# Exponentials in sixteen pieces with the maximum as bias, and masks on ScalarE, in layers 0 and 2 of a four-layer graph attention kernel

## The chip, the core and the metric

The kernel runs on one core of a Trainium2 chip. The metric is the time of one launch on the device, in microseconds (us). A core has five engines with a queue each: TensorE (PE in the profile; its weight loads are PEld), VectorE (DVE), ScalarE (ACT), GpSimd (POOL) and SyncE (SP, which here only issues transfers). Each engine works through its own queue in order and waits on semaphores for the others. All data here are float32 but for the masks, which are bytes.

## The reference

The input x holds 128 graphs of 64 nodes with 512 features; adj says which nodes are neighbours. Four layers follow each other, each on relu(layernorm(x)) and each added to x. Layers 0 and 2 are the same function with their own weights: four heads of 64, attention limited to neighbours.

```python
def _L0_gnn_ref(x, adjacency_mask, Wq, Wk, Wv, Wo, bo):
    q = split_heads(x @ Wq)
    k = split_heads(x @ Wk)
    v = split_heads(x @ Wv)
    sim = jnp.einsum('bhid,bhjd->bhij', q, k) * scale          # scale = 64 ** -0.5 = 0.125
    neg = -jnp.finfo(sim.dtype).max
    sim = jnp.where(adjacency_mask[:, None, :, :], sim, neg)
    attn = jax.nn.softmax(sim, axis=-1)
    out = jnp.einsum('bhij,bhjd->bhid', attn, v)
    return out @ Wo + bo
...
h = jnp.maximum(_layernorm(x, axis=-1), 0.0)
x = x + _L0_gnn_ref(h, adj, L0_gnn_Wq, L0_gnn_Wk, L0_gnn_Wv, L0_gnn_Wo, L0_gnn_bo)
```

Layer 1 is such an attention with eight heads, a second layernorm and a mask that always keeps the diagonal. Layer 3 multiplies the softmax by a mask of cosine similarities over 0.1 and uses eight heads; its last stage is another. The change touches neither's arithmetic.

## The kernel before, in words

**Tiles and steps.** The 8192 rows (graph, node) are cut into 16 steps of 512 rows: four blocks of 128 rows, each holding two graphs of 64 nodes. The kernel runs over layer by layer, and within a layer step by step, so there are 64 (layer, step) pairs. Between layers x lies in DRAM.

**Stages of one step of layer 0 or 2.** SP loads x into `xin` (L486). `scales` and `normalize` make the layernorm: DVE takes statistics (L443, L445), adds epsilon (L448), POOL takes the power -1/2 (L450), DVE makes the bias (L452), ACT applies it (L459). PE transposes 128x128 squares into `ptr` (L570) and ACT copies them into `hT` (L574). Products with weights are done by Strassen's scheme in Winograd's form (`winograd`): seven products of half-size blocks instead of eight, with sums of blocks made ahead (`sums_of_b`, L363 on DVE and L366 on POOL). All its matmuls stand at L613, into the PSUM banks `mA`, `mB` and `mC`. What comes out of a bank is taken away by `Out` or `Residual`: ACT copies (L630, L650, and L1040 into a buffer `u`), DVE adds (L643, L654), POOL adds (L1045). A product may overwrite a bank only once the copy out of it is done, so PE waits for such copies.

**The attention.** `scores` (L930) multiplies the heads' q and k in 64x64 quarters into the tile `sc`, which fills two PSUM banks: 128 partitions (two graphs of 64 queries) by 1024 (16 groups of 64 keys: four heads, four blocks). Then `softmax_parts`:

- DVE overwrites the non-neighbours with a very negative number (L941, a predicated copy whose mask is the tile `n`, with 1 where there is no edge);
- DVE takes the maximum of each group of 64 (L947) into `mx`, 128x16;
- DVE subtracts it (L949) from the scores into the SBUF tile `E`; with this `sc` is free (`se.set()`);
- ACT takes exp(0.125 E) in place, one operation of 1024 (L952);
- DVE sums each group (L959), takes the reciprocal (L963), and POOL multiplies (L965).

`transposed` turns `E` (eight ACT copies at L974 and one DVE transpose at L979), `attention` multiplies it by v into `po` (L1097). The scores `sc` and `po` share one buffer of two PSUM banks (`r_sc`, a ring of 1), so po of one step can be written only once `sc` of the next is released. ACT copies `po` out (L1106), DVE makes the sums for the product with `Wo` (L363), and the seven products of `Wo` are added to `xres`, which holds x plus the bias vector (L1024), and stored (L1065).

**Masks.** `masks` runs once for each step: SP loads 128x256 bytes of adj (L988); in layers 0 and 2 DVE makes `n` = (adj == 0) at L1005. Layer 1 also takes out the diagonal (L1002), layer 3 has another form (L996).

**What sets the order.** No queue is written by hand. Every stage is a Python generator that yields what its next instruction will cost, for example `yield dve(1.2)` or `yield act(1.06)`, before it records it. The class `Order` keeps a clock for each engine and always lets the generator go on whose instruction can start first by these figures. Two rules bend this: streams carry a priority, and on ACT and DVE a stream of priority 0 (the copies that empty PSUM banks) that would become ready before a longer operation ends goes ahead of it (`urgent`). So the figures in the yields fix the order of the instructions on every engine; the chip then runs each queue in that order, and where real lengths differ from the figures an instruction waits in its place. A changed figure or a new operation can thus move instructions everywhere.

Rings and banks limit how far a stage can run ahead: `E` has two buffers, adj and `n` two each, the small tile pool `soft` (for `mx` and the sums) three, `u` four, `xres` two, `mA` and the pair `mB`/`mC` two each.

**Lines that the change and the prediction touch:** `softmax_parts` (L934 to L955), `masks` (L983 to L1007), `softmax` (L1191), and around them L443 to L459 (layernorm), L613 (matmuls), L630, L650, L1040 (ACT copies), L643 (DVE adds), L1045 and L366 (POOL), L486, L988, L1020 (loads by SP).

Of the kernel before, what the change touches and what calls it, by code (L numbers as in the profile page):

```python
# [8 lines left out]
F32 = mybir.dt.float32  # L9
U8 = mybir.dt.uint8  # L10
AF = mybir.ActivationFunctionType
ALU = mybir.AluOpType
AX = mybir.AxisListType

P = 128
D = 512
N = 64
# [194 lines left out]
def dve(us):  # L212
    return ("dve", us, 0.1)


def act(us):
    return ("act", us, 0.1)
# [6 lines left out]
def load(us=2.2):  # L224
    return ("sp", 0.6, us)
# [3 lines left out]
def gnn_stack(ctx: ExitStack, tc: tile.TileContext, a: dict, out: bass.AP):  # L229
    nc = tc.nc  # L230
# [12 lines left out]
    const = ctx.enter_context(tc.tile_pool(name="const", bufs=1))  # L243
# [43 lines left out]
    sel = const.tile([P, 32], F32, name="sel")  # L287
    nc.vector.memset(sel, 0.0)

    bdw = const.tile([P, P], F32, name="bdw")  # L290
    nc.vector.memset(bdw, 0.0)
    for g in range(2):
# [638 lines left out]
                                         lT[r, c, k], rT[r, c, k], start=True, stop=True)  # L931
        return S, e

    def softmax_parts(S, se, E, mask, neg, masked):  # L934

        m = mask.rearrange("p b k -> p (b k)")
        n = m.shape[1]
        sv = S.rearrange("p a (c m) -> p (a c) m", m=n)
        shape = [P, 1024 // n, n]
        yield dve(1.5)  # L940
        nc.vector.copy_predicated(sv, m[:, None, :].to_broadcast(shape),  # L941
                                  negs[:, neg:neg + 1, None].to_broadcast(shape))
        masked.set()
        S3 = S.rearrange("p a (i k) -> p (a i) k", k=N)
        mx = soft.tile([P, 16], F32, tag="mx", name="mx")
        yield dve(1.2)
        nc.vector.tensor_reduce(mx, S3, AX.X, ALU.max)  # L947
        yield dve(1.2)
        nc.vector.tensor_tensor(E, S3, mx[:, :, None].to_broadcast([P, 16, N]), ALU.subtract)  # L949
        se.set()  # L950
        yield act(1.06)
        nc.scalar.activation(E, E, AF.Exp, scale=0.125)  # L952
        sm = soft.tile([P, 2, 16], F32, tag="sm", name="sm")
        yield from row_sums(sm[:, 0, :], E)
        return sm  # L955

    def row_sums(o, E):
        yield dve(1.2)
        nc.vector.tensor_reduce(o, E, AX.X, ALU.add)  # L959

    def divide(E, sm):
        yield dve(0.24)
        nc.vector.reciprocal(sm, sm)  # L963
        yield pool(1.95)
        nc.gpsimd.tensor_mul(E, E, sm[:, :, None].to_broadcast([P, 16, N]))  # L965
# [17 lines left out]
    def masks(l, s):  # L983

        adj, ae = yield from r_adj.new()
        n = TB * N
        yield load(3.5)
        nc.sync.dma_start(adj.rearrange("p b k -> p (b k)"), a["adj"][:, s * n:(s + 1) * n])  # L988
        n0, ne = yield from r_n0.new()
        if l == 3:  # L990
            nz = small.tile([P, TB], U8, tag="nz", name="nz", bufs=1)
            yield dve(0.3)
            nc.vector.tensor_scalar(nz, adj[:, :, 0], 0.0, None, ALU.is_equal)

            yield dve(0.6)
            nc.vector.scalar_tensor_tensor(n0, adj, 0.0, nz[:, :, None].to_broadcast([P, TB, N]),  # L996
                                           ALU.is_equal, ALU.mult)
            return adj, ae, n0, ne
        yield dve(0.6)
        if l == 1:  # L1000

            nc.vector.scalar_tensor_tensor(n0, adj, 0.0, noteye[:, None, :].to_broadcast(  # L1002
                [P, TB, N]), ALU.is_equal, ALU.mult)
        else:
            nc.vector.tensor_scalar(n0, adj, 0.0, None, ALU.is_equal)  # L1005
        ae.set()
        return n0, ne, None, None  # L1007
# [150 lines left out]
    def front(l, s):  # L1158

        mask, me, nf, nfe = yield from masks(l, s)  # L1160
        yield s_ready[l, s]
        z = st[l, s]
# [6 lines left out]
        for u, blocks in enumerate(units):  # L1169
            E, e = yield from r_e.new("E")  # L1170
            S, se = yield from scores(z["q"], z["k"], 2 * nch, blocks)
            if u == len(units) - 1:
                for n in ("q", "k", "qk"):
                    if f"{n}_done" in z:
                        z[f"{n}_done"].set()
            m = mask[:, blocks[0]:blocks[0] + len(blocks)]
            z["e", u], z["exp", u] = (E, e), od.event()
            od.spawn(softmax(l, z, u, S, se, m, masked[u]), 1)
# [11 lines left out]

    def softmax(l, z, u, S, se, m, masked):  # L1191
        E = z["e", u][0]
        sm = yield from softmax_parts(S, se, E, m, (0, 1, 0, 2)[l], masked)
        z["sm", u] = sm
        if l < 3:
            yield from divide(E, sm[:, 0, :])
            z["e_ready", u].set()
        z["exp", u].set()
# [136 lines left out]
```

## Time and profile before

| | us |
|---|---|
| median of three runs (lowest, highest) | 2790.13 (2788.91, 2795.86) |
| the profiled execution, its own time | 2791.22 |
| its span, from the first to the last instruction | 2789.2 |
| layer 0 without its start and end: window 40 to 470 | 430 |
| layer 1: window 510 to 1300 | 790 |
| layer 2: window 1385 to 1850 | 465 |
| layer 3: window 1900 to 2700 | 800 |

The granted clock of TensorE in this execution is 0.993 of full speed. The DMA engines are busy between a tenth and a half of the time in each fortieth of the span.

How to read the views: the busy totals give, for each engine, the time in which it worked, the share of the span and the number of instructions. The chain of work that ended last is followed back from the last instruction, each time to what released it. A group's row names line, engine, operation, output and input, their shapes and the number of instructions; then the busy time, the mean length of one in ns, and the idle time of the engine just before them with what ended it. The view of waits says who waited for whom: us in total, how often, the longest. The windows give the busy time of each engine within a stretch; the last three columns there are the granted clock, the share of the DMA engines and GB/s. In the timeline the columns are the start, the length, the engine, and in square brackets the idle time before with its releaser.

### The profile page before, as it was taken

Reading aid. Unit: us, or ns where it says so; the run is one execution under the profiler, and the core shown is the slowest. Engines: PE = TensorE matmul, PEld = TensorE weight load, DVE = VectorE, ACT = ScalarE, POOL = GpSimd, SP = SyncE. Lnnn points to the kernel's source line nnn. Section 1 sums busy time; section 2 is a strip of 40 time slices with the busy share of each in tenths; the row PEclk is TensorE's granted clock in tenths of the full one; section 3 lists DMA queues with packets and bytes.
Section 4 is the critical chain, followed back from the end, with each engine's and each line's share of the span. In section 5 each row is a group of like instructions: output and inputs, shape, how many; then the busy total and the mean of one; then the engine's idle time right before and its main releaser. Section 6 shows DMA issues by size and latency. Waiting matters only on the chain.

```text
span 2789.2 us, 63654 instructions
## 1 busy us (share of the span) xinstructions
PE 2723.9 (98%) x26728; PEld 2362.1 (85%) x26728; DVE 1896.2 (68%) x2780; ACT 1872.4 (67%) x3149; POOL 1608.2 (58%) x1242
## 2 busy tenths in 40 slices
PE   8999999999999999999999999999999999999997
PEld 7888888888888888888888888878888888888876
DVE  6766767677767667766657666746777667776656
ACT  5756756688777777776656656657566776677644
POOL 5667667645435445446656576676665656555543
PEclk9999999999999999999999999999999999999998
DMA  4333333212112111112322242332422233223221
GB/s 157 108 107 109 108 116 114 96 63 77 47 62 77 47 61 64 61 47 97 122 93 92 93 138 93 108 104 78 111 64 63 71 93 86 64 63 84 73 63 47
DMA packets 160430, 238.51 MB, mean 86 GB/s; under 512 B 23952, under 2 KB 69008, under 8 KB 160144
## 3 DMA queue, kind: packets, MB, share of 16 engines
q1 hardware_dynamic: 145632, 219.98, 25.4%
q10 hardware_dynamic: 14512, 14.47, 1.6%
q8 instruction: 210, 3.44, 0.5%
q14 instruction: 76, 0.62, 0.1%
HBM read 166.77 MB, written 67.63 MB: 84 GB/s over the span
## 4 chain that ended last, share of the span: by engine, by line
PE 91%; DVE 4%; POOL 2%; ACT 1%; issue 1%; DMA 1%; POOLq 0%; SPq 0%; ACTq 0%; DVEq 0%
PE mA L613 46%; PE mC L613 23%; PE mB L613 12%; PE sc L930 5%; PE po L1097 2%; PE ptr L570 2%; PE po L1242 1%; PE mmn L872 1%; POOL xres L1045 1%; POOL xres L1024 1%; ACT F L974 1%; DVE xres L643 1%; DVE E L949 0%; DVE t L363 0%; POOL E L965 0%
## 5 line engine op out<-in xcount | busy, mean ns | idle before, releaser
L974 ACT COPY F<-E 32x512 f32<-32x512 f32 x768 | 472.5, 615 | 41.0 <-POOL E L965 26.3
L1045 POOL TENSOR_TENSOR xres<-xres,u 128x512 f32<-128x512 f32 x192 | 259.9, 1361 | 296.3 <-ACT u L1040 236.1
L1024 POOL TENSOR_TENSOR xres<-xres,u 128x512 f32<-128x512 f32 x192 | 260.8, 1380 | 23.0 <-DMA xres<-x 17.0
L366 POOL TENSOR_TENSOR t<-hT 128x512 f32<-128x512 f32 x126 | 181.4, 1440 | 145.7 <-DVE hT L544 89.0
L459 ACT ACTIVATE xin<-xin,rs 128x512 f32<-128x512 f32 x320 | 247.8, 810 | 19.4 <-DVE rs L452 15.6
L630 ACT COPY v<-mA 128x256 f32<-128x256 f32 (+1 forms) x192 | 92.0, 479 | 218.5 <-PE mA L613 205.5
L534 ACT COPY t<-xin 32x512 f32<-32x512 f32 x364 | 224.1, 616 | 6.4
L450 POOL TENSOR_TENSOR rs<-rs,mhalf 128x2 f32<-128x2 f32 x160 | 115.9, 726 | 192.0 <-DVE rs L448 168.7
L443 DVE BATCH_NORM_STATS2 st<-xin 128x6 f32<-128x512 f32 x320 | 214.9, 672 | 15.8 <-DMA xin<-in_x 7.7
L613 PE MATMUL mA<-w_vo,t 128*128 128x128 f32 (+1 forms) x1152 | 204.5, 312 | 1.1 <-ACT u L1040 1.1
L613 PE MATMUL mA<-t,w_qk 128*128 128x256 f32 x768 | 185.9, 381 | 1.5 <-DVE t L363 1.5
L965 POOL TENSOR_TENSOR E<-E,sm 128x1024 f32<-128x1024 f32 x64 | 127.8, 1997 | 100.6 <-DVE sm L963 87.3
L613 PE MATMUL mA<-t,w_q 128*128 128x256 f32 x744 | 179.2, 383 | 0.0
L613 PEld LDWEIGHTS mA<-w_vo,t 128*128 128x128 f32 x1152 | 166.2, 191 | 14.6 <-ACT u L1040 4.3
L613 PE MATMUL mA<-t,w_k 128*128 128x256 f32 x744 | 177.3, 381 | 0.0
L366 POOL TENSOR_TENSOR t<-hT,t 128x512 f32<-128x512 f32 x126 | 168.3, 1336 | 7.7 <-DVE hT L544 4.2
L959 DVE TENSOR_REDUCE sm<-E 128x16 f32<-128x1024 f32 x128 | 154.9, 1210 | 12.8 <-ACT E L952 12.1
L613 PEld LDWEIGHTS mA<-t,w_qk 128*128 128x128 f32 x768 | 144.4, 192 | 20.3 <-DVE t L363 1.7
L613 PEld LDWEIGHTS mA<-t,w_q 128*128 128x128 f32 x744 | 140.5, 191 | 20.8 <-issue 1.2
L613 PEld LDWEIGHTS mA<-t,w_k 128*128 128x128 f32 x744 | 140.3, 190 | 19.4
L979 DVE STREAM_TRANSPOSE pt<-F 128x1024 f32<-128x1024 f32 x96 | 118.7, 1236 | 49.8 <-ACT F L974 49.6
L1040 ACT COPY u<-mA 128x512 f32<-128x512 f32 x144 | 84.4, 586 | 97.7 <-PE mA L613 88.8
(217 smaller groups left out, 6908.9 us busy)
## 6 DMA issues: line engine op xcount, KB each, us to landing
x<-xres SPq DMA_DIRECT2D x96, 512.0 KB
xin<-x SPq DMA_DIRECT2D x96, 512.0 KB
xres<-x SPq DMA_DIRECT2D x64, 512.0 KB
xres<-in_x SPq DMA_DIRECT2D x32, 512.0 KB
u<-rs SPq DMA_DIRECT2D x128, 128.0 KB
xres<-x SPq DMA_DIRECT2D x64, 256.0 KB
out<-xres SPq DMA_DIRECT2D x64, 256.0 KB
xin<-in_x SPq DMA_DIRECT2D x30, 512.0 KB
```

What stands on the lines that cost most here:

```text
L366: nc.gpsimd.tensor_tensor(o, i0, i1, ALU.subtract)
L443: nc.vector.bn_stats(st, v[:, t, :])
L459: nc.scalar.activation(v[:, t, :], v[:, t, :], func, bias=rs[:, 2, t:t + 1], scale=rs[:, 0, t:t + 1])
L534: nc.scalar.copy(o, v)
L613: nc.tensor.matmul(o, l, r, start=(first and m == 0 and k == 0), stop=(k == KC - 1), skip_group_check=True)
L930: nc.tensor.matmul(S[g * N:(g + 1) * N, par, col], lT[r, c, k], rT[r, c, k], start=True, stop=True)
L959: nc.vector.tensor_reduce(o, E, AX.X, ALU.add)
L965: nc.gpsimd.tensor_mul(E, E, sm[:, :, None].to_broadcast([P, 16, N]))
L974: nc.scalar.copy(F[g * N + 32 * k:g * N + 32 * (k + 1), :, 32 * i:32 * (i + 1)], E[g * N + 32 * i:g * N + 32 * (i + 1), :, 32 * k:32 * (k ...
L979: nc.vector.transpose(o, F)
L1024: nc.gpsimd.tensor_add(xr[:, t, :], xr[:, t, :], bo[l])
L1045: nc.gpsimd.tensor_add(v, v, both(u))
```

## The change

In layers 0 and 2, and only there:

- the subtraction of the maximum is left out. Instead the maximum is multiplied by -0.125 in place (128x16), and ACT takes exp(0.125 S - 0.125 max) straight from the scores' banks, in 16 operations of 64 columns each, since a bias is one number for each partition and each group of 64 has its own. The scores' banks are released after the last of these;
- the mask is made by ACT as 1 - adj, with a bias tile `ones` and scale -1, instead of by DVE's comparison.

The figures given to the planner are 0.1 for the scaling, 0.21 for each exp and 0.4 for the mask.

```diff
+    ones = const.tile([P, 1], F32, name="ones")
+    nc.vector.memset(ones, 1.0)
...
-    def softmax_parts(S, se, E, mask, neg, masked):
+    def softmax_parts(S, se, E, mask, neg, masked, narrow=False):
...
         nc.vector.tensor_reduce(mx, S3, AX.X, ALU.max)
-        yield dve(1.2)
-        nc.vector.tensor_tensor(E, S3, mx[:, :, None].to_broadcast([P, 16, N]), ALU.subtract)
-        se.set()
-        yield act(1.06)
-        nc.scalar.activation(E, E, AF.Exp, scale=0.125)
+        if narrow:
+            yield dve(0.1)
+            nc.vector.tensor_scalar(mx, mx, -0.125, None, ALU.mult)
+            for i in range(16):
+                yield act(0.21)
+                nc.scalar.activation(E[:, i, :], S3[:, i, :], AF.Exp, bias=mx[:, i:i + 1], scale=0.125)
+            se.set()
+        else:
+            yield dve(1.2)
+            nc.vector.tensor_tensor(E, S3, mx[:, :, None].to_broadcast([P, 16, N]), ALU.subtract)
+            se.set()
+            yield act(1.06)
+            nc.scalar.activation(E, E, AF.Exp, scale=0.125)
...
+        if l != 1:
+
+            yield act(0.4)
+            nc.scalar.activation(n0, adj, AF.Identity, bias=ones, scale=-1.0)
+            ae.set()
+            return n0, ne, None, None
         yield dve(0.6)
         if l == 1:
...
-        sm = yield from softmax_parts(S, se, E, m, (0, 1, 0, 2)[l], masked)
+        sm = yield from softmax_parts(S, se, E, m, (0, 1, 0, 2)[l], masked, l in (0, 2))
```

The branch for layer 3 in `masks` returns before the new one, so `l != 1` there means layers 0 and 2. The matmuls, their number and their operands are the same in both kernels.

## The prediction

> **What bounds the kernel now.** I read the busy totals and the chain first, then the windows by layer, then what the tensor engine (PE) waits for in layers 0 and 2, then the rows of the operations that the change touches, and last one step of the timeline.
>
> Busy totals and the chain that ended last, from the page:
>
> ```profile
> PE 2723.9 (98%) x26728; PEld 2362.1 (85%) x26728; DVE 1896.2 (68%) x2780; ACT 1872.4 (67%) x3149; POOL 1608.2 (58%) x1242
> ...
> PE 91%; DVE 4%; POOL 2%; ACT 1%; issue 1%; DMA 1%; POOLq 0%; SPq 0%; ACTq 0%; DVEq 0%
> ```
>
> PE is idle for 65 us in all. The change removes no matmul, so it can win only what PE stands idle, and only in layers 0 and 2. Those windows (layer 0, layer 1, layer 2; columns: length, then busy us and count for PE, weight loads, DVE, ACT, POOL):
>
> ```profile
> 40.00:470.00 430.00, 420.67 (x4128) 375.57 (x4127) 306.63 (x484) 281.45 (x476) 290.40 (x225) 1.00 0.34 111
> ...
> 510.00:1300.00 790.00, 789.70 (x7153) 683.55 (x7152) 546.80 (x813) 610.96 (x945) 383.65 (x318) 1.00 0.19 63
> ...
> 1385.00:1850.00 465.00, 451.23 (x4285) 401.62 (x4287) 310.95 (x491) 287.62 (x492) 298.14 (x233) 0.99 0.31 105
> ```
>
> PE idles 9.3 us in the layer 0 window and 13.8 us in the layer 2 window, 23.1 us together: 0.72 us for each of 32 steps. Who ends those waits (0 to 480 us, then 1300 to 1880 us):
>
> ```profile
> PE mC L613 <- DVE xres L643: 3.6, 2, 1.8
> PE mB L613 <- DVE xres L643: 2.6, 2, 1.3
> PE po L1097 <- DVE E L949: 2.4, 3, 1.0
> ```
>
> ```profile
> PE mC L613 <- DVE xres L643: 5.3, 2, 3.5
> PE po L1097 <- DVE pt L979: 3.0, 2, 2.8
> PE po L1097 <- DVE E L949: 2.5, 3, 1.1
> ```
>
> Only the L949 lines (4.9 us) are the operation that the change takes away. ACT is 62 to 65% busy there, DVE 67 to 71%: neither is a bound, so only order and lateness matter. Groups of the operations concerned, shapes apart:
>
> ```profile
> L949 DVE TENSOR_TENSOR E<-sc,mx 128x1024 f32<-128x1024 f32 x96 | 117.0, 1219 | 1.8
> L952 ACT ACTIVATE E<-E 128x1024 f32<-128x1024 f32 x96 | 101.5, 1057 | 9.4 <-DVE E L949 8.9
> L634 ACT ACTIVATE kT<-mA,vecs 128x256 f32<-128x256 f32 x96 | 40.3, 471 | 27.6 <-PE mA L613 26.7
> L448 DVE TENSOR_SCALAR rs<-mv 128x2 f32<-128x2 f32 x160 | 66.2, 414 | 5.0
> L1005 DVE TENSOR_SCALAR n<-adj 128x256 uint8<-128x256 uint8 x32 | 17.5, 547 | 1.3 <-DMA adj<-in_adj 1.3
> ```
>
> One softmax of layer 0 in the timeline (start, length):
>
> ```profile
> 163.56 0.37 ACT L630 COPY v<-mA 128x256 f32<-128x256 f32 x1 [0.18 <-PE mA L613]
> 163.83 1.52 ACT L459 ACTIVATE xin<-xin,rs 128x512 f32<-128x512 f32 x2
> 164.68 1.23 DVE L941 COPY_PREDICATED sc<-n,negs 128x1024 f32<-128x1024 uint8 x1 [1.77 <-PE sc L930]
> 165.95 1.22 DVE L947 TENSOR_REDUCE mx<-sc 128x16 f32<-128x1024 f32 x1
> 167.44 1.22 DVE L949 TENSOR_TENSOR E<-sc,mx 128x1024 f32<-128x1024 f32 x1
> ```
>
> ACT's next instruction starts 0.27 us after a 0.37 us copy: lengths overlap by 0.1, so occupancy is read from starts.
>
> **What the Trainium skill says.** "ScalarE: Activation LUTs", What ACT_TABLE_LOAD costs: an ACTIVATE takes 186 ns + 0.833 ns per element, each pointer operand (here the bias) adds about 93 ns, and back-to-back ones overlap by about 93 ns. The trace agrees on slope ((586-372)/256 = 0.836 ns, copies of 512 and 256) and overlap. "SBUF — State Buffer", Who interferes with whom: a tensor_scalar in a two-port mode and GpSimd exclude each other for a whole instruction. The trace agrees: L448 takes 0.17 us in the median and up to 1.85, L1005 0.285 and up to 1.28. "PSUM — Partial Sum Buffer", Engine vs sequencer instructions: ScalarE's queue is strict first in, first out, so an exp that waits holds every copy behind it.
>
> **The change part by part**, per step, 16 steps in each of two layers.
>
> 1. The subtraction goes: DVE -1.22 us. Also its 4.9 us of PE waits.
>
> 2. One exp of 1024 (length 1.06, occupancy about 0.95) becomes 16 of 64 out of PSUM with a bias. No row shows that. L634 is the nearest: pointer bias, PSUM, 256 wide, two in 0.84 us, so 0.84-0.47 = 0.37 us apart. Less 192 x 0.836 ns: 0.21 us. Upper end: if they don't overlap, 0.471-0.160 = 0.31. I take 0.21, because the pairs of L634 do overlap: 3.4 us, or ACT +2.4 us. At 0.31 it is 5.0.
>
> 3. The maximum is scaled by -0.125: one TENSOR_SCALAR on 128x16. From L448: 0.17 alone, up to about 1.3 if POOL has just begun an operation (its rows here last 1.3 to 1.4). It lies between maximum and first exp.
>
> 4. The mask moves to ACT: DVE -0.55 (mean of L1005), ACT +0.4 (256 x 0.833 ns and, by the page, two times 93 ns; 0.5 if nothing overlaps).
>
> 5. The scores' bank stays held until the last exp instead of the end of the subtraction (4.0 us after the scores: 168.66-164.62).
>
> Sum: ACT +2.8 us per step, 90 us in all; DVE about -1.4 per step. At some 28.4 us per step ACT goes to about 75%. Nothing of this is on PE by itself; what counts is the order.
>
> The kernel's planner lays every queue out anew, and the new order repeats identically over 24 of the 32 steps (11 in layer 0, 13 in layer 2); layers 1 and 3 keep theirs but at their edges. So I follow one repeating step with measured lengths, zero at the end of the scores. PE start to start: product of Wo 0.87, of V 0.89, scores or po 1.09 (timeline: 179.08 to 179.94, 165.04 to 165.93, 163.46 to 164.55). After the scores PE runs five Wo products and half a V product to 4.80, the other half to 5.25, then the last Wo product, four V products and half of one to 10.12, then po. Results are readable about 0.2 later.
>
> ACT after the scores: two copies of u, exp x2, copy u (fifth Wo product, readable 4.1), mask, exp, copy V, exp x10, copy V, exp, copy V, exp x2. PE's last Wo product, due at 5.25, waits for that third u, which is now **behind two exps**, and these behind the scaled maximum.
>
> DVE: predicated copy 0.1 to 1.4; then xres<-mB, which by its semaphore waits for POOL's addition of the first u, which stands behind a POOL sum of hT; then maximum, then scale. POOL: sum to about 0.3, addition to 1.6, so xres 1.7 to 2.4, maximum to 3.6; scale waits for POOL's operation then running, to about 4.3; first exp 4.45. Then u is copied 4.9 to 5.45: PE stalls **0.2 us**. If the predicated copy (two SBUF inputs, 1.2 to 2.3 us in its rows) and POOL's addition take turns instead, the addition ends at 2.8, the maximum at 4.8, the scale at 5.5; first exp 5.6, u at 6.6: **1.35 us**. Both ends are open; I take the middle, 0.75.
>
> Behind it, from the first exp e: V copies are due at PE's pace, and ten exps at 0.21 put the second at e+3.9, where its product is readable at e+3.85; the last exp ends at e+5.5, po's turn is e+5.9. So part 5 and the long exp run cost nothing at 0.21. At 0.31 the ten cost 1.0 us more, of which 0.27 is slack: 0.75 us of stall.
>
> The mask's wait: SP issues its load 0.9 us behind that of xin, which waits for the last transposes, about -1.9. Halves of xin land 3.6 to 4.6 and 4.9 to 5.9 us after issue in layer 2 (1454.95 to 1458.55 and 1459.88; 1771.58 to 1776.13 and 1777.45), so the mask's data is there by about 4.5; ACT gets there at 5.4. Cover 0.9 us; without it the copies of V wait.
>
> At the very start ACT's table load (1.28) and a mask (0.5) now precede the two loads of the second step's x on ACT's queue: 1.8 us later. Their first reader is at 13.35 against an issue at 3.58; cost 0 to 1.5, taken as 0.5.
>
> Sum: 24 x 0.75 = 18.0, the 8 irregular steps as before 8 x 0.72 = 5.8, start 0.5, less the 23.1 that these windows lose now: **+1.2 us**. The profiled execution took 2791.2 us (span 2789.2), 1.1 above the median of the runs shown (2790.1); from the median: about 2791, and I say 2792.
>
> **Rivals.**
> - *Late or dear exps (slower).* One mechanism: ACT's copies queue behind exps. With the first exp at 5.6: 24 x 1.35 + 5.8 + 0.5 - 23.1 = +15.6, 2806. With exps 0.31 apart as well, 24 x 0.75 more: 2824. It decides from a stall of about 1.05 us per repeating step (24 x 1.05 + 6.3 - 23.1 = +8.4). For: POOL is busy just then, L448's 1.85. Against: L634's pairs.
> - *The mask's load is late on ACT's queue (slower).* Each us beyond the 0.9 of cover stalls about 1 us: 0.5 us in 24 steps gives +12, 2803. For: xin and masks share SP's queue. Against: the mask was awaited only once (1.3 us).
> - *Old stalls vanish (faster).* Stall 0.2, irregular steps half as bad: 4.8 + 2.9 - 23.1 = -15, 2775. For: DVE relieved by 1.4 us, and most waits above end on DVE. Against: L643 waits for POOL, which isn't relieved.
>
> **How the numbers follow.** No change 0.38 (own range 2782 to 2798), exps 0.30, mask 0.06, old stalls vanish 0.26. About 0.3% (8.4 us) is what a measurement of this kernel can tell from no change. Faster 0.26, same 0.38, slower 0.36. Range 2775 to 2820: it cuts off only the far ends of the fast and dear cases.
>
> **What would show it.** Right: 512 exps of 64 with starts 0.21 apart; L952's row down to 64; ACT's busy time up by 90 (by starts) to 141 us (by lengths: 32 x (16 x 0.31 - 1.06) + 16); PE idle in the two windows near 24 us, its waits named after ACT u. Scale row at 0.2 to 1.3. Wrong: starts 0.3 apart; PE waiting for exp at po; ACT idle before the mask with a DMA as releaser; or PE idle under 10 us there.

## The result, and the profile after

| | us |
|---|---|
| before, median of five runs (lowest, highest) | 2792.41 (2788.91, 2795.86) |
| after, median of five runs (lowest, highest) | 2776.12 (2772.56, 2778.84) |
| ratio, with its 95% interval | 0.9941 [0.9926, 0.9955] |
| span of the profiled executions, before and after | 2789.2, 2770.7 |

The change makes the kernel 0.6% faster. The forecast was 2792, with "no change" as the likeliest case; the measured time lies at the lower end of the forecast range of 2775 to 2820.

Busy totals and the chain that ended last, from the page of after:

```profile
PE 2716.6 (98%) x26728; PEld 2357.8 (85%) x26728; DVE 1900.5 (69%) x2749; ACT 1955.6 (71%) x3661; POOL 1611.8 (58%) x1242
...
PE 94%; DVE 2%; ACT 2%; issue 1%; POOL 0%; DMA 0%; POOLq 0%; ACTq 0%; SPq 0%; DVEq 0%
```

PE is still the bound, and the chain now lies on it for 94% instead of 91%. ACT took 83 us more work. DVE, which the change was to relieve, works as long as before (1896.2, now 1900.5). Of the 18.5 us by which the span is shorter, 7.3 are PE's busy time and 11.2 its idle time. The same three windows as before the change, same columns:

```profile
40.00:470.00 430.00, 424.59 (x4161) 379.40 (x4163) 313.27 (x470) 322.42 (x731) 293.48 (x226) 1.00 0.33 112
510.00:1300.00 790.00, 787.71 (x7118) 681.27 (x7110) 543.33 (x811) 608.32 (x940) 377.09 (x314) 1.00 0.19 64
1385.00:1850.00 465.00, 459.93 (x4399) 410.63 (x4398) 321.42 (x487) 328.91 (x728) 321.98 (x249) 1.00 0.33 113
```

PE idles 5.4 and 5.1 us in layers 0 and 2, 10.5 instead of 23.1. Whom it waits for in these two windows (layer 0, then layer 2):

```profile
PE mA L615 <- ACT u L1056: 4.4, 10, 0.5
PE po L1113 <- ACT E L955: 0.9, 1, 0.9
PE mC L615 <- ACT v L632: 0.7, 1, 0.7
```

```profile
PE mA L615 <- ACT u L1056: 4.5, 10, 0.5
PE mA L615 <- ACT m L636: 0.3, 1, 0.3
```

The old waits for DVE (`xres`, `E` and `pt`) are gone. In their place is one that returns in nearly every repeating step: PE waits for a copy of `u` out of bank `mA`. The other lines stand for one wait each. The groups of the operations that the change touches, shapes apart:

```profile
L955 ACT ACTIVATE E<-sc,mx 128x64 f32<-128x64 f32 x512 | 122.9, 349 | 34.8 <-DVE mx L952 34.8
L943 DVE COPY_PREDICATED sc<-n,negs 128x1024 f32<-128x1024 uint8 x64 | 110.9, 1733 | 99.8 <-PE sc L932 99.8
L952 DVE TENSOR_SCALAR mx<-mx 128x16 f32<-128x16 f32 x32 | 19.0, 594 | 1.0
L1012 ACT ACTIVATE n<-adj,ones 128x256 uint8<-128x256 uint8 x32 | 16.7, 523 | 0.0
```

ACT stood idle before the exps for 34.8 us in all, for the scaled maximum; before the mask it never did (0.0). The timeline of one repeating step of layer 0, with only the lines of the scores' softmax and of the product of Wo beside it (start, length):

```profile
168.29 2.32 DVE L943 COPY_PREDICATED sc<-n,negs 128x1024 f32<-128x1024 uint8 x1 [2.75 <-PE sc L932]
170.52 0.68 DVE L645 TENSOR_TENSOR xres<-mB,xres 128x512 f32<-128x512 f32 x1
171.12 1.21 DVE L949 TENSOR_REDUCE mx<-sc 128x16 f32<-128x1024 f32 x1
172.37 0.62 DVE L952 TENSOR_SCALAR mx<-mx 128x16 f32<-128x16 f32 x1
173.02 0.61 PE L615 MATMUL mA<-w_vo,hT 128*128 128x128 f32 x4
173.02 0.52 ACT L955 ACTIVATE E<-sc,mx 128x64 f32<-128x64 f32 x2 [1.39 <-DVE mx L952]
173.43 0.58 ACT L1056 COPY u<-mA 128x512 f32<-128x512 f32 x1
174.07 1.13 PE L615 MATMUL mA<-w_vo,t 128*128 128x256 f32 x4 [0.44 <-ACT u L1056]
...
174.76 2.19 ACT L955 ACTIVATE E<-sc,mx 128x64 f32<-128x64 f32 x10
```

Read it from below: the last Wo product (174.07) waits for the copy of `u` (173.43), this stands behind two exps (173.02), these wait for the scaled maximum (172.37), and this ends a run of DVE operations whose first, the predicated copy, took 2.32 us.

So the predicted stall is there, yet the kernel is faster. Two things were changed at once: the operations, and, through the planner's figures, the order of nearly every queue. The experiments separate them.

### The profile page after: what moved, and what is told of

Its sections match the earlier page's. It is cut to its first block, busy times and chain, and to the rows that moved or that the text cites. A ratio compares the mean times of both kernels' runs of the same rounds, so it can differ in the third digit from the quotient of the medians.

```text
span 2770.7 us, 64129 instructions
## 1 busy us (share of the span) xinstructions
PE 2716.6 (98%) x26728; PEld 2357.8 (85%) x26728; DVE 1900.5 (69%) x2749; ACT 1955.6 (71%) x3661; POOL 1611.8 (58%) x1242
## 4 chain that ended last, share of the span: by engine, by line
PE 94%; DVE 2%; ACT 2%; issue 1%; POOL 0%; DMA 0%; POOLq 0%; ACTq 0%; SPq 0%; DVEq 0%
PE mA L615 47%; PE mC L615 24%; PE mB L615 12%; PE sc L932 5%; PE po L1113 2%; PE ptr L572 2%; PE po L1258 1%; ACT F L984 1%; PE mmn L874 1%; ACT u L1056 0%; ACT E L955 0%; DVE mx L949 0%; DMA xin<-in_x 0%; POOL v L847 0%; DVE v L656 0%
## 5 line engine op out<-in xcount | busy, mean ns | idle before, releaser
L1061 POOL TENSOR_TENSOR xres<-xres,u 128x512 f32<-128x512 f32 x192 | 250.1, 1309 | 218.7 <-ACT u L1056 197.5
L1040 POOL TENSOR_TENSOR xres<-xres,u 128x512 f32<-128x512 f32 x192 | 264.7, 1404 | 2.8 <-issue 2.2
L368 POOL TENSOR_TENSOR t<-hT,t 128x512 f32<-128x512 f32 x126 | 182.5, 1448 | 9.0 <-DVE hT L546 4.2
L943 DVE COPY_PREDICATED sc<-n,negs 128x1024 f32<-128x1024 uint8 x64 | 110.9, 1733 | 99.8 <-PE sc L932 99.8
L955 ACT ACTIVATE E<-sc,mx 128x64 f32<-128x64 f32 x512 | 122.9, 349 | 34.8 <-DVE mx L952 34.8
```

The lines of the kernel that those rows point to most:

```text
L368: nc.gpsimd.tensor_tensor(o, i0, i1, ALU.subtract)
L955: nc.scalar.activation(E[:, i, :], S3[:, i, :], AF.Exp, bias=mx[:, i:i + 1], scale=0.125)
L1040: nc.gpsimd.tensor_add(xr[:, t, :], xr[:, t, :], bo[l])
L1061: nc.gpsimd.tensor_add(v, v, both(u))
```

## The experiments

Each ratio is to the kernel before, run on the same chip.

**Operations and order, apart.** The planner places an instruction by its yield and by when buffers are marked as free, whatever the instruction does, so old operations can be put behind new yields. Old operations in the new order (PE, POOL and SP get the same instructions in the same order as after; the scores' banks are still released behind the exp):

```diff
         if narrow:
             yield dve(0.1)
-            nc.vector.tensor_scalar(mx, mx, -0.125, None, ALU.mult)
+            nc.vector.tensor_tensor(E, S3, mx[:, :, None].to_broadcast([P, 16, N]), ALU.subtract)
             for i in range(16):
                 yield act(0.21)
-                nc.scalar.activation(E[:, i, :], S3[:, i, :], AF.Exp, bias=mx[:, i:i + 1], scale=0.125)
+                if i == 15:
+                    nc.scalar.activation(E, E, AF.Exp, scale=0.125)
...
             yield act(0.4)
-            nc.scalar.activation(n0, adj, AF.Identity, bias=ones, scale=-1.0)
+            nc.vector.tensor_scalar(n0, adj, 0.0, None, ALU.is_equal)
```

> Theory O (the order): the changed kernel is faster because its queues were laid out anew into a step that repeats, whichever operations fill it. Theory D (DVE's load): it is faster because the subtraction and the mask left DVE. Here every queue has the changed kernel's order, but the old operations stand in it: the subtraction in place of the scaling on DVE, one exp of 1024 in place of the sixteenth piece on ACT, and the mask on DVE. O: as fast as the changed kernel, 2766 to 2778 us, and the third copy of u no longer stands behind exps, so the 20 waits of PE for it (8.9 us) should be gone and the time nearer 2767. D: 2787 or more, since DVE does its old work again.

And new operations with the old figures, which give nearly the order of before. It isn't quite the same, because the scores' banks are now released behind the exps and the planner reckons with that:

```diff
         if narrow:
-            yield dve(0.1)
+            yield dve(1.2)
             nc.vector.tensor_scalar(mx, mx, -0.125, None, ALU.mult)
+            yield act(1.06)
             for i in range(16):
-                yield act(0.21)
                 nc.scalar.activation(E[:, i, :], S3[:, i, :], AF.Exp, bias=mx[:, i:i + 1], scale=0.125)
...
-            yield act(0.4)
+            yield dve(0.6)
             nc.scalar.activation(n0, adj, AF.Identity, bias=ones, scale=-1.0)
```

> The converse: the changed kernel's operations (scaling, sixteen exps, mask on ACT), but the planner is told the old figures (1.2 for what stands in place of the subtraction, 1.06 for all exps together, 0.6 on DVE for the mask), so that the order is nearly that of the kernel before. O: no gain, 2788 or more, and slower than before by what 3.5 us of exps in a slot of 1.06 hold up (32 x up to 1 us: up to 2825). D: 2770 to 2782, since DVE is relieved just as in the changed kernel.

Medians in us, with the ratio to before:

| | order of before | order of after |
|---|---|---|
| old operations | 2789.6 (before) | 2757.4, 0.9884 [0.9871, 0.9896] |
| new operations | 2830.0, 1.0141 [1.0125, 1.0157] (nearly this order) | 2776.1, 0.9941 [0.9926, 0.9955] (after) |

The order gains 32 us with the old operations. The new operations cost in either order. In the old it is 40 us, the small difference in order included. In the new it is 18.7 by the medians, 16 by the ratios (0.9941 less 0.9884, of 2790; the two kernels were compared with different runs of before) and 14.6 by the profiled spans. The busy totals of the page and the windows of layers 0 and 2, old operations in the new order:

```profile
PE 2712.8 (98%) x26728; PEld 2357.2 (86%) x26728; DVE 1932.0 (70%) x2781; ACT 1867.3 (68%) x3149; POOL 1614.8 (59%) x1242
```

```profile
40.00:470.00 430.00, 429.37 (x4256) 385.75 (x4255) 332.29 (x494) 286.21 (x489) 303.08 (x232) 1.00 0.35 116
...
1385.00:1850.00 465.00, 463.54 (x4348) 414.35 (x4346) 329.55 (x493) 293.04 (x511) 326.52 (x253) 1.00 0.32 111
```

PE idles 0.6 and 1.5 us there, with DVE busy for 36 us more in all than before the change. So a fuller DVE hurts nothing, and its relief is not what made the kernel faster. The other corner, new operations with the old figures, PE's waits in layer 0:

```profile
PE po L1113 <- ACT E L955: 9.8, 6, 2.0
PE mB L615 <- DVE xres L645: 4.5, 2, 2.2
PE mC L615 <- DVE xres L645: 3.6, 2, 1.8
```

In the old order po comes too soon for sixteen exps, and the old waits for `xres` stay.

**The stall alone.** After, but with the first two exps recorded together with the third, behind the copy of `u` and the mask; only ACT's queue differs:

```diff
             for i in range(16):
                 yield act(0.21)
-                nc.scalar.activation(E[:, i, :], S3[:, i, :], AF.Exp, bias=mx[:, i:i + 1], scale=0.125)
+                for j in ([], [], [0, 1, 2])[i] if i < 3 else [i]:
+                    nc.scalar.activation(E[:, j, :], S3[:, j, :], AF.Exp, bias=mx[:, j:j + 1], scale=0.125)
```

> The changed kernel with one thing moved: on ACT the first two exps stand behind the third copy of u and the mask, next to the third exp; all other queues are the same. Theory U (all that the new operations cost in the new order is the wait of PE for that copy): its 20 waits go, the repeating step falls from 29.43 to about 28.7 us, and the time to 2757 to 2761. Rival B (the longer hold of the scores' bank and ACT's longer exps cost on their own): the waits only change their name, to copies of V or to po behind the last exp, and the time stays at 2766 to 2776.

2759.6 us, 0.9886 [0.9871, 0.9901]. All but 2.2 us of what the new operations cost in this order is that one wait. Its windows:

```profile
40.00:470.00 430.00, 428.95 (x4251) 385.06 (x4250) 320.42 (x476) 326.62 (x734) 303.23 (x232) 1.00 0.36 116
...
1385.00:1850.00 465.00, 464.31 (x4358) 415.40 (x4356) 321.65 (x481) 330.89 (x733) 326.50 (x252) 1.00 0.33 112
```

PE idles 1.1 and 0.7 us, with the sixteen exps and the mask still on ACT. From start to start of the scores a repeating step of after takes 29.43 us (19 of them; a twentieth, the last of layer 0, is longer by as much, and three more take 29.08). Here and with the old operations it takes 28.72. The 0.71 us of difference is more than the 0.44 that the view of waits shows; the timeline of the old operations in the new order says why (to be set against 173.02, 174.07 above):

```profile
170.03 0.61 PE L615 MATMUL mA<-w_vo,hT 128*128 128x128 f32 x4
170.47 1.03 PE L615 MATMUL mA<-w_vo,t 128*128 128x256 f32 x4
171.34 1.05 PE L615 MATMUL mB<-w_vo,hT 128*128 128x128 f32 x8
```

Without a wait the second product starts 0.44 us after the first, 0.17 before the first ends; in after it starts 1.05 later, which is 0.61 late. The next starts 0.96 later instead of 0.87 (175.03 in after), another 0.09. Together 0.70: matmuls overlap when nothing holds them up, the idle time of the view starts only at the modelled end of the one before the wait, and the overlap that is lost at both ends of the wait is counted as busy. That is where a part of PE's busy time goes.

**The mask and the exps alone.** After with its mask made by DVE (order unchanged: `yield act(0.4)` stays):

```diff
             yield act(0.4)
-            nc.scalar.activation(n0, adj, AF.Identity, bias=ones, scale=-1.0)
+            nc.vector.tensor_scalar(n0, adj, 0.0, None, ALU.is_equal)
```

> The changed kernel in its own order with the mask made by DVE again, in the same place; the exps stay narrow. U: the third copy of u is still behind two exps, so 2774 to 2778, as the changed kernel. If the mask on ACT costs or saves anything of its own, the time differs from the changed kernel by up to 24 x 0.4 = 10 us: 2766 or 2786.

2777.0, 0.9947 [0.9933, 0.9962], against 2776.1 of after: in this order it doesn't matter which engine makes the mask. Then the exps without the mask's branch (`if l != 1: ...` in `masks` left out), and the mask without the exps (`l in (0, 2)` in `softmax`'s call left out), each with the order that its own yields give:

> Only the exps from the scores' banks, masks on DVE as before, planned anew. D: a part of the gain in proportion to DVE's relief, 0.6 of 1.2 us net per step against 1.2 for both parts: 2780 to 2784. O: no proportion to the relief; anything from 2770 to 2800 by how the planner happens to lay the steps, with PE's waits telling which: near 10 us of idle in layers 0 and 2 if the step repeats without waits, 20 or more if it is ragged.

> Only the masks on ACT, softmax as before, planned anew. D: DVE is relieved by 0.55 us per step: 2782 to 2788. O: not in proportion, 2775 to 2800, by the order.

The exps alone give 2784.6, 0.9982 [0.9974, 0.9989]; the mask alone 2792.7, 1.0009 [0.9999, 1.0018]. −5 and +2.5 us don't add up to −16: each part changes the order of everything, so the parts can't be priced one by one.

**Is any new order a better one?** Two kernels with before's operations and one changed figure each: `yield act(0.95)` instead of `act(1.06)` for the exp, and 0.28 instead of 0.6 for the masks of layers 0 and 2:

```diff
-        yield act(1.06)
+        yield act(0.95)
         nc.scalar.activation(E, E, AF.Exp, scale=0.125)
```

```diff
-        yield dve(0.6)
+        yield dve(0.6 if l == 1 else 0.28)
         if l == 1:
```

> The kernel before with the same operations; only the planner's figure for the exp is 0.95, its occupancy read from starts, instead of 1.06. Theory O (a new layout moves the time by itself): the time moves by 3 us or more to either side, 2765 to 2815, and PE's waits in layers 0 and 2 change in number and place. Theory D (operations decide): 2787 to 2793, as before.

> The kernel before with the same operations; only the planner's figure for the mask on DVE in layers 0 and 2 is 0.28, its shortest length, instead of 0.6. O: moves by 3 us or more to either side, 2770 to 2810. D: 2787 to 2793.

2791.1, 1.0000 [0.9992, 1.0008], and 2796.3, 1.0023 [1.0017, 1.0030]. No: of these two new orders one brings nothing and the other a little loss.

**Which of the change's figures make the good order?** Old operations throughout, and one feature of the new order after the other. First the banks released only behind the exp (this one edit holds for all four layers, those below for layers 0 and 2 alone):

```diff
         nc.vector.tensor_tensor(E, S3, mx[:, :, None].to_broadcast([P, 16, N]), ALU.subtract)
-        se.set()
         yield act(1.06)
         nc.scalar.activation(E, E, AF.Exp, scale=0.125)
+        se.set()
```

> The old operations with the old figures; only the planner is told that the scores' bank comes free after the exp instead of after the subtraction. Which of the change's figures makes the repeating step is open. If it is the later release of the bank (po planned later): a repeating step near 28.7 us and 2757 to 2765. If not: ragged steps as before, 2783 to 2798.

Then also 16 times `act(0.21)` for the exp's place, the one exp recorded in the last, with `dve(1.2)` for the subtraction; and the same with `dve(0.1)`; the mask as before in both:

```diff
-            yield dve(0.1)
+            yield dve(1.2)
             nc.vector.tensor_tensor(E, S3, mx[:, :, None].to_broadcast([P, 16, N]), ALU.subtract)
             for i in range(16):
                 yield act(0.21)
                 if i == 15:
                     nc.scalar.activation(E, E, AF.Exp, scale=0.125)
             se.set()
```

> The old operations; the planner is told 16 x 0.21 for the exp (and the bank free after it), but the old 1.2 for the subtraction and 0.6 on DVE for the mask. If the length of ACT's slot makes the repeating step: near 28.7 us and 2757 to 2765. If the short figure on DVE (0.1) or the mask's slot on ACT is needed: 2770 to 2795.

> The old operations in the order of the run with narrow exps alone (figures 0.1 and 16 x 0.21, mask on DVE at 0.6). Theory U: that run's step alternated between 28.6 and 29.5 us; if its longer half was PE waiting for copies behind exps, it falls to 28.7 each, 32 x 0.4 = 13 us less than that run's 2784.6: 2769 to 2774. If the longer half lies in the layout: 2780 to 2785.

Idle time of PE in us in four stretches of each trace (window less PE's busy time), and the median:

| old operations with | 40:450 | 450:1400 | 1400:1770 | 1770:1920 | median | ratio |
|---|---|---|---|---|---|---|
| figures of before | 9.3 | 3.2 | 8.9 | 5.7 | 2789.6 | 1 |
| banks held to the exp | 6.9 | 3.3 | 6.6 | 4.5 | 2784.5 | 0.9981 [0.9973, 0.9989] |
| and a long place for the exp | 0.0 | 8.1 | 5.9 | 1.6 | 2776.2 | 0.9949 [0.9935, 0.9962] |
| and a short one on DVE | 0.0 | 14.3 | 0.0 | 1.4 | 2774.5 | 0.9942 [0.9930, 0.9955] |
| and the mask's place on ACT (all of after's) | 0.6 | 2.5 | 0.0 | 1.6 | 2757.4 | 0.9884 [0.9871, 0.9896] |

The long place for the exp is what clears layer 0's repeating steps and the passage from layer 2 to 3. The short one on DVE clears those of layer 2, but the passages from layer 0 to 1 and from 1 to 2 (second column) grow worse. The mask's place on ACT clears these: 12 us of idle time, where the median falls by 17. No single figure makes the order. Why the planner, given these figures, arrives at steps without a wait was not followed further and stays open.

The row with 2774.5 has the order of the kernel with the exps alone (PE, POOL and SP get the same instructions in the same order). That kernel took 2784.6, so there the order gained 15 us and the sixteen exps gave 10 of it back. The new operations lose time in all three orders in which they were compared.

The last row is the fastest kernel of the study: before's operations in after's order, 0.7% below after (2757.4 / 2776.1 = 0.993).

**Another cost of a wait.** From before to after PE's busy time fell by 7.3 us though it runs the same matmuls, and with the old operations in the new order by 11.1. The granted clock has a part in that. The traces hold stretches of 3.41 us (or twice that) in which it is 0.50. Two of them from before, in layer 2 and in its passage to layer 3, each behind the 3.41 us that precede it (the last three columns are the granted clock, the DMA share and GB/s):

```profile
1442.84:1446.25 3.41, 0.81 (x53) 0.81 (x57) 2.54 (x4) 0.00 (x0) 3.33 (x4) 1.00 0.32 118
1446.25:1449.66 3.41, 3.41 (x34) 2.93 (x26) 1.75 (x6) 2.78 (x4) 1.90 (x3) 0.50 0.87 297
1831.97:1835.38 3.41, 0.33 (x2) 0.30 (x3) 1.60 (x2) 2.04 (x5) 3.33 (x3) 1.00 0.00 0
1835.39:1838.79 3.40, 3.40 (x12) 2.75 (x11) 0.00 (x0) 0.21 (x1) 1.33 (x2) 0.50 0.00 0
```

PE is idle for 2.6 and 3.1 us, and directly behind that its clock is halved, although it now works without a pause. In each of the thirteen traces the starts of these stretches lie whole multiples of 3.41 us apart. The traces have 62 drops, and before every one of them PE stood idle for at least 1.80 of the 3.41 us. In the 10,335 pieces of this length at full clock that have no drop behind them, the idle time is at most 1.94 us. So in these traces a wait of about half a piece or more that falls within one piece is followed by half the clock in the next. A wait of the same length that falls across two pieces need not be, and that is a matter of where it happens to lie. No run moved a wait on purpose to test this.

Leaving out the last 21 us or so of each kernel, before has six such drops, after one, the old operations in the new order two, the new operations with the old figures eight. With PE's busy time in them taken as half lost, an estimate, they cost 9.7, 1.7, 3.4 and 14.9 us.

## Why the prediction was wrong

By its own steps:

- **What bounds it.** Right: PE does, and what is won is won from its waits, though not from their idle time alone.
- **Part 1, the subtraction.** The 4.9 us of waits for L949 went, but in the new order they go with the subtraction kept as well. DVE, forecast at 1.4 us less per step (45 us), worked 4.3 us more: the new order by itself gave it 36 us (1896.2 to 1932.0), among it the predicated copies, which take 1732 ns on average instead of 1493. Against it the new operations took off 31.5. Its fuller queue costs nothing by itself: in the two windows no wait of PE names DVE now. But the stall hangs on DVE at one remove, through the exps that wait for the scaled maximum.
- **Part 2, sixteen exps.** Right: ten of them take 2.19 us, and neighbours start 0.20 us apart (the median of 362 pairs), where 0.21 was worked out from L634. The Trainium skill, "ScalarE: Activation LUTs", What ACT_TABLE_LOAD costs, lets back-to-back ones overlap by about 93 ns. Here they overlap by more, some 150 ns (349 of length less the 197 between starts). ACT's busy time rose by 83 us, a little under the 90 to 141 expected.
- **Part 3, the scaled maximum.** Right: 0.17 to 1.08 us, 0.62 in the median, for a forecast of 0.17 to 1.3. The first exp starts 4.87 us after the scores' end at 168.15, between the forecast's 4.45 and 5.6.
- **Part 4, the mask.** Right in that its load was never late (0.0 us of idle time ahead of it), and which engine makes it is worth 0.9 us, within the spread of the runs.
- **The stall.** Its place was right: the order's new wait is the third copy of `u` behind two exps. Its size came near with some luck: 0.71 us in 20 repeating steps and 0.36 in three, 15.3 us in all, for a forecast of 24 x 0.75 = 18.0. That 0.75 was the middle between two courses, and neither was taken: POOL's addition kept its 1.27 us (168.25 to 169.52), and the predicated copy beside it stretched to 2.32. Old and new operations in the same order differ by 14.6 us in the spans of their profiled executions and by 18.7 in the medians (that execution of after is the fastest of its five).
- **The step that failed is the sum:** "24 x 0.75 = 18.0, the 8 irregular steps as before 8 x 0.72 = 5.8, start 0.5, less the 23.1 that these windows lose now: +1.2 us". Three of its terms failed, the first most of all.
  - *The 23.1*, what the old order loses, was read as PE's idle time in two windows. With the same operations in a better order the span is 33.1 us shorter (2789.2 to 2756.1). Of that only 22.0 us is idle time of PE (65.3 to 43.3), and 21.0 of these lie in the two windows, so the idle time was read rightly. The other 11.1 us is busy time that waits bring with them. By the estimate above 6.3 of it (9.7 less 3.4) is the halved clock; the 4.8 left over is most likely lost overlap, as in the stall, but it wasn't traced wait by wait. From start to start it could have been seen: the scores of before return in a cycle of seven steps, of 206.5 us in layer 0 (136.68 to 343.18) and 208.2 in layer 2 (1567.99 to 1776.18). That is 29.50 and 29.74 us for a step, 0.78 and 1.02 above the 28.72 of the new order, where the prediction had 0.72. Over 16 steps each it is 28.9 us. So one side of the sum, the stall, was priced from start to start, and the other by the view's idle time; the two don't count the same.
  - *The 5.8* for irregular steps was carried over from before's mean. In the new order they lose next to nothing: with the stall taken away PE idles 1.7 us in the two windows.
  - *The start's 0.5* had the wrong cause. The loads were to be issued 1.8 us later, behind the table load and the mask. They were issued at 3.66 us, against 3.58 before:

```profile
3.58 1.28 ACT L1012 ACT_TABLE_LOAD   x1 [3.58 <-issue]
3.66 1.05 ACTq L488 DMA_DIRECT2D xin<-in_x  x2
```

  What the first steps do lose is 1.3 us: behind the first scores they take 23.20 and 23.54 us, with the old operations in the same order 22.22 and 23.23. PE's waits there name the exps (`po` for `E`, 0.9 us) and a copy of `v` on ACT's queue (0.7 us).

  With 33.1 for 23.1, 15.3 for 18.0, 1.3 for 0.5 and nothing for 5.8 the sum is 15.3 + 1.3 - 33.1 = -16.5. The spans, from which the 33.1 comes, differ by -18.5; that the medians differ by -16.3 is a chance agreement.
- **The rivals.** "Old stalls vanish", 2775, had the time and only half the reason: the old waits did vanish, but its "For", DVE's relief, fell (in the fastest kernel DVE works 36 us more than before), and its stall of 0.2 was too small. "Late or dear exps" names what really costs in the new order, at less than its 1.05 us per step. The mask's load didn't come late.
- **What would show it.** PE's idle time of 10.5 us in the two windows fell far from the 24 expected, and just above the 10 named as a sign of being wrong. That its waits would be named after ACT's `u` came true (8.9 of the 10.5 us).

## What to carry to other kernels

Where a planner orders the queues by figures, a change to an operation is two changes: run the old operations behind the new figures, and the new ones behind the old, before giving the operation the credit. Here the order gained 32 us, and the operations gave 15 to 19 of it back, nearly all through one copy that stood behind two early exps. When a new order may repeat without the old one's waits, price the old waits from start to start of a whole cycle: their idle time alone told 22 us of 33, and the rest stood in the profile as PE's busy time.

## What the runs showed of the hardware

- A wait of PE costs more than its idle time: 0.44 us shown, 0.71 us of step, in 20 such steps.
- The granted clock of this kernel on one core fell to 0.50 for 3.41 or 6.83 us, and for 20 to 24 us at the end. All 62 drops in thirteen traces came right behind 3.41 us in which PE idled for 1.80 us or more; at full clock and without a drop behind it the most was 1.94.
- The predicated copy of 128x1024 grew from 1493 to 1733 ns in the mean by order alone (1732 with the old operations in the new order). In after, POOL was at work all through the 30 of 64 that took over 1.8 us, and not at all beside 16 of the 28 shortest (under 1.4 us). The row of before, to be set against that of L943 above:

```profile
L941 DVE COPY_PREDICATED sc<-n,negs 128x1024 f32<-128x1024 uint8 x64 | 95.6, 1493 | 34.2 <-PE sc L930 34.2
```

- An exp of 128x64 out of PSUM with a bias for each partition takes 349 ns by length, and the next in a row starts 0.20 us later.
